# Sparse attention and graph convolution on one core: hub lookups, table scatters, tile clearing and short row blocks placed elsewhere in the order of work

## The chip, the core and the metric

The kernel runs on one core of a Trainium2 chip. Times are microseconds (us) of device time for one whole execution. The engines of the core are called PE (TensorE, matmul), DVE (VectorE), ACT (ScalarE), POOL (GpSimd) and SP (SyncE, which only issues transfers here). A time is the median of several executions; a profile is of one execution, whose own time is given beside its span.

## The reference, cut to what matters

There are 2708 rows of 1024 numbers, and a 0/1 matrix adj of 2708 x 2708 whose density falls with row and column, so that a few rows and columns at the front have many ones and some rows have none. All values are float32.

```
def layer0(x, adj):                       # attention over the ones of adj
    q, k, v = x @ W_q.T + b_q, x @ W_k.T + b_k, x @ W_v.T + b_v
    z = (q @ k.T) / sqrt(1024) * adj
    z = where(z == 0, -10000, z)
    return relu(softmax(z, axis=1) @ v)
def layer1(x, adj):
    return adj @ (x @ weight) + bias
x   = layernorm(x + layer0(x, adj))
out = layernorm(x + layer1(x, adj))
```

A row without ones gets the softmax of equal scores, which is the mean of all rows of v.

## The kernel before

**Numbers rather than masks.** The kernel never forms the full matrix of scores. With M the product of Wq and Wk, the score of row i and column j is a dot product of y_i = x_i M with x_j, so only the columns in a row's list are needed. The kernel builds those lists, sorts the rows by their number of columns into 22 blocks (NB) of up to 128 rows (the last block has 20), and for each block gathers column after column: one gather brings, for each of the 128 rows, the row of x which is its next column. Row blocks with long lists come first; the longest lists (the "hub") are cut into shares, which are worked on as a block of their own and joined later. Families: blocks 0 to 7 are the first family (FAMILY = 8) and 8 to 21 the second; each has its own table of lists in memory. The table of a family is written by scatters, one for each block of records (`records_out`, L650), and loaded back into the tile `tabs` (L660); `records_back` (L677) then makes the masks from it.

**The hub's lists.** `deal_hub` (L455 to L582) is a generator that is advanced a step at a time (`next(deal)`, L754 to L755) among the first y blocks. One of its steps looks up the hub's columns: 11 small gathers write the tile `found` (L566 to L568). The next one makes `valid_h`, `tab_h` and `less_h` from it (L570 to L574), and two permutation tiles `to_0` and `far_0` which don't depend on it (L576 to L581). Small tiles such as `found` and `at_i` come from the pool `lists`, which is given back before the tiles of the attention are laid out; pools that are laid out over it have to wait for the last use of what was there.

**Stages.** (1) Until about 150 us: M, and the lists of columns from adj. (2) The y blocks: `y_block` (L367) multiplies one block of 128 rows with M, in 16 matmuls of 128x512 (two halves of 8), and DVE adds a row `y_bc` while it empties each PSUM bank into `yo` (L320, called from L377). There are four such banks. SP stores `yo` to memory as `y_d` (L365). Blocks 0 to 7 stand in a first loop (L749), with lists and hub work between them; blocks 8 to 21 are the first steps of the list `steps` (L1129). The last block has its own form, `y_last` (L398). (3) Pairs: `steps` goes on with ten pairs of row blocks, whose weighted sums of x rows are turned (transposed on PE, L823) and multiplied with Wv by a seven-product scheme (`pair_products`, products at L306). (4) Layer 1 from about 764 us: sums of gathered rows of the new x (`sum_rows`, L1280), turned and multiplied with the layer's weights in ten `units`, with a normalisation and a scatter of the result (L810) one unit later.

**Attention jobs.** They are worked on beside the y blocks and pairs. A job (`attend` L918; `attend_one` L983; for the hub and block 0 `attend_shares` L1011) gathers the rows of y that belong to its block (`yg`, L428), which for the first family needs all of blocks 0 to 7 stored, then gathers x rows into a ring of nine tiles `g` (L434), makes one score per gathered tile on DVE (L904), a softmax, and the weighted sum `r` of the same tiles (first term on ACT at L959 or L1043, others on DVE at L961 or L1045). A tile of `g` is free again when its term of the sum is done. Because a gather leaves a lane alone where a row's list is shorter, the nine tiles are cleared once (L793 to L794) before their first use.

**What sets the order.** Each engine works its queue strictly in the order in which the program was laid out; there is one queue for POOL's gathers, scatters and loads. The order is set by a loop over `steps` (L1173) that keeps a credit of estimated time (`COST`, L1131) and advances jobs while there is credit. Parts under `tc.high_priority` are put ahead of ordinary ones by the scheduler. `follow(later, earlier)` (L421) makes one instruction wait for another; `products` holds the last matmul of every y block in the order of issue, so that `products[-2]` is the end of the block before the one issued last. `join` (L1152) advances hub and block 0 to their last steps, PE work at L1053 and L1063, a given number of steps after their sums are issued.

**The mean of x.** Rows without columns need the mean of all rows of x. `column_sums` (L415) makes it from the transposed x tiles on ACT, eight sums for each block, each behind one of that block's matmuls; `y_last` adds them up (`xbT`, L404 and L405), and `bcast_rows` (L1215) spreads the result over the partitions with transposes at L187.

**Rows without columns in layer 1.** The blocks named `last` (20 and 21) consist of such rows. In layer 1 they need only their own row of x1 plus the bias (`gather_x1`, L1301), a normalisation and a scatter (`finish1`, L1308); both are appended at i == 2 (L1365) and finished at the next unit, in the loop over units (L1352). The sum of the hub takes 11 gathers at i == 4 (L1363), behind those of the unit three further on.

## Time and profile before

| | |
|---|---|
| median of three runs | 1101.32 us (1097.92 to 1105.58) |
| profiled execution, own time | 1093.68 us |
| its span | 1092.0 us |
| PE busy | 983.0 us (90%) |
| DVE busy | 824.4 us (75%) |
| POOL busy | 484.5 us (44%) |
| ACT busy | 426.0 us (39%) |
| y matmuls (L374), busy | 300.8 us |
| scores (L904), 108 of them | 131.7 us, 1.219 us each |
| gathers of g in the attention (L434), 84 of them | 112.3 us, 1.337 us each |

A busy PE is not a PE at its peak, and the shares are averages over stages with different limits. In the lists of waits below, an engine and its line come first, then what ended the wait, then the sum of the waits in us, their number and the longest one. In timelines, each line is a start, a duration, the engine, the line of the kernel, the operation and its tiles; the bracket at the end gives the idle time just before it and what ended it. "issue" there means that the engine waited for nothing that the profile shows. The table by stretch gives the length of the stretch, then for each of PE, weight load, DVE, ACT and POOL the busy time and the number of instructions, then the granted clock, the share of the transfer engines and GB/s.

### The profile page before, as it was taken

To read this page: it belongs to the slowest core of one execution; us is meant where nothing else is said; L and a number is where in the kernel's file an instruction comes from. 1 tells how busy PE (TensorE), PEld (TensorE's weight loads), DVE (VectorE), ACT (ScalarE), POOL (GpSimd) and SP (SyncE) were. 2 spreads that over 40 slices of the span, in tenths; PEclk is the share of its full clock that TensorE was granted. 3 is DMA by queue.
4 is the path that set the end of the run, shared out by engine and by line. 5 is a ranking of instruction groups with operands and counts; after the bars stand their busy time and mean duration, and the time that the engine had idled before them with its cause. 6 is when DMAs were issued, how large, how long until landed. Compare 5 with 4: busy or idle time off the path is not lost.

```text
span 1092.0 us, 10690 instructions
## 1 busy us (share of the span) xinstructions
PE 983.0 (90%) x2761; PEld 463.0 (42%) x2761; DVE 824.4 (75%) x2038; ACT 426.0 (39%) x893; POOL 484.5 (44%) x530
## 2 busy tenths in 40 slices
PE   7999989999997999659999999999499885999993
PEld 6444444444333434225554444444244332445441
DVE  8999799953387998995799999645478865696532
ACT  4599994222032322222623444322322334333421
POOL 0000500057554555442465765110678776787400
PEclk9999989999999999889999999999799996999997
DMA  9688849956576867453447777225597697879711
GB/s 347 191 286 250 251 143 326 314 175 209 176 256 207 271 201 226 137 165 119 131 131 232 259 233 269 78 77 206 170 314 225 183 302 243 259 225 312 192 50 42
DMA packets 105781, 228.79 MB, mean 210 GB/s; under 512 B 22500, under 2 KB 49900, under 8 KB 105710
## 3 DMA queue, kind: packets, MB, share of 16 engines
q0 software_dynamic: 48192, 147.52, 42.5%
q1 hardware_dynamic: 57518, 80.50, 22.7%
q8 instruction: 23, 0.38, 0.1%
q14 instruction: 48, 0.39, 0.1%
HBM read 217.60 MB, written 33.68 MB: 230 GB/s over the span
## 4 chain that ended last, share of the span: by engine, by line
PE 28%; issue 19%; DVE 17%; POOL 12%; DMA 9%; ACT 1%; POOLq 0%; DVEq 0%; SPq 0%
PE po L306 23%; POOL g L434 6%; DVE junkv L904 2%; DMA g<-in_x_dram,tabs 2%; PE po L374 2%; DVE r L961 2%; POOL xr L428 1%; PE tr L823 1%; DMA g<-x_d,tabs 1%; POOL yg L428 1%; POOL tab_d L652 1%; DMA out_dram<-t,tabs 1%; DVE junkc L738 1%; DMA yg<-y_d,tabs 1%; DVE at_a L235 1%
## 5 line engine op out<-in xcount | busy, mean ns | idle before, releaser
L374 PE MATMUL po<-m,xt 128*128 128x512 f32 x672 | 300.8, 607 | 17.2 <-DVE yo L320 14.9
L374 PEld LDWEIGHTS po<-m,xt 128*128 128x128 f32 x672 | 128.7, 194 | 184.2 <-issue 153.9
L904 DVE SCALAR_TENSOR_TENSOR junkv<-yg,g 128x1024 uint8<-128x1024 f32 x108 | 131.7, 1219 | 44.8 <-DMA yg<-y_d,tabs 25.9
L306 PE MATMUL po<-t,s_all 128*128 128x512 f32 x320 | 148.2, 607 | 10.1 <-DVE xr L320 8.8
L434 POOL DMA_INDIRECT g<-in_x_dram,tabs x84 | 112.3, 1337 | 76.6 <-DVE r L961 19.0
L1295 DVE SCALAR_TENSOR_TENSOR r<-g,valid,r 128x1024 f32<-128x1024 f32 x77 | 98.0, 1280 | 29.2 <-DMA g<-x_d,tabs 26.7
L700 PE MATMUL po<-wk_o,wq_o 128*128 128x512 f32 x256 | 110.5, 592 | 0.0
L306 PEld LDWEIGHTS po<-t,s_all 128*128 128x128 f32 x320 | 61.2, 193 | 91.7 <-issue 72.8
L434 POOL DMA_INDIRECT g<-x_d,tabs x66 | 79.1, 1199 | 22.5 <-issue 16.8
L306 PE MATMUL po<-w,rT 128*128 128x512 f32 x160 | 74.2, 605 | 14.3 <-DVE t L1332 14.3
L417 ACT ACTIVATE junka<-xt 128x128 f32<-128x128 f32 x176 | 54.2, 308 | 82.2 <-PE po L374 61.5
L235 DVE FIND_INDEX8 at_a<-ones,a 128x8 uint16<-128x83 f32 (+3 forms) x132 | 82.6, 630 | 0.3 <-issue 0.3
L866 ACT ACTIVATE junks<-t,lnm 128x1024 uint8<-128x1024 f32 (+1 forms) x40 | 45.9, 1147 | 94.3 <-DVE lnm L864 93.1
L961 DVE SCALAR_TENSOR_TENSOR r<-g,pr,r 128x1024 f32<-128x1024 f32 x64 | 81.5, 1279 | 1.4 <-ACT r L959 1.2
L824 ACT COPY rT<-tr 128x512 f32<-128x512 f32 x76 | 41.2, 588 | 98.4 <-PE tr L823 97.7
L700 PEld LDWEIGHTS po<-wk_o,wq_o 128*128 128x128 f32 x256 | 48.3, 190 | 59.3 <-issue 58.6
L306 PE MATMUL po<-t,rT 128*128 128x512 f32 x160 | 73.0, 598 | 0.3 <-DVE t L320 0.3
L306 PE MATMUL po<-w,s_all 128*128 128x512 f32 x160 | 72.1, 592 | 0.0
L306 PE MATMUL po<-wv,s_all 128*128 128x512 f32 x160 | 71.9, 592 | 0.0
L306 PE MATMUL po<-wv,rT 128*128 128x512 f32 x160 | 70.7, 594 | 0.0
L879 ACT ACTIVATE t<-t,nmr,rstd 128x1024 f32<-128x1024 f32 (+1 forms) x40 | 49.0, 1238 | 49.5 <-DVE nmr L878 48.4
L810 POOL DMA_INDIRECT x_d<-t,tabs x22 | 25.9, 1175 | 75.0 <-ACT t L879 62.8
(352 smaller groups left out, 1425.8 us busy)
## 6 DMA issues: line engine op xcount, KB each, us to landing
xt<-in_xT_dram SPq DMA_DIRECT2D x21, 512.0 KB
y_d<-yo SPq DMA_DIRECT2D x21, 512.0 KB
a<-in_x_dram SPq DMA_DIRECT2D x21, 512.0 KB
a<-in_adj_dram SPq DMA_DIRECT2D x21, 413.5 KB
a<-in_adj_dram SPq DMA_DIRECT2D x21, 338.5 KB
a<-in_adj_dram SPq DMA_DIRECT2D x21, 263.5 KB
wq_i<-in_wqT_dram SPq DMA_DIRECT2D x8, 512.0 KB
wk_i<-in_wkT_dram SPq DMA_DIRECT2D x8, 512.0 KB
```

What stands on the lines that cost most here:

```text
L235: nc.vector.max_index(at[:n, i], ones[:n, :8], a[:n, cuts[i] + 8 * i:cuts[i + 1] + 8 * i + 8])
L306: put = nc.tensor.matmul(acc, a[:, k], w[:, k], start=start and k == 0, stop=stop and k == DC // 2 - 1, skip_group_check=True)
L374: put = nc.tensor.matmul(po, xts[b][:, c, :], m_q[c // 4][h][:, c % 4], start=(c == 0), stop=(c == DC - 1))
L417: put = nc.scalar.activation(junka, xts[b][:, c, :], AF.Copy, accum_out=xs[:, c, b:b + 1])
L434: nc.gpsimd.indirect_dma_start(out=dst[:n], out_offset=None, in_=src, in_offset=bass.IndirectOffsetOnAxis(ap=at, axis=0), bounds_check=N - ...
L700: nc.tensor.matmul(po, wq_o[i // 2][:, o, i % 2 * P:(i % 2 + 1) * P], wk_o[:, o, hs], start=(o == 0), stop=(o == DC - 1))
L824: nc.scalar.copy(rT[:, g * 4:g * 4 + 4, :], tr)
L866: nc.scalar.activation(junks[:n], t[:n], AF.Square, bias=nm[:n], accum_out=vs[:n])
L879: applied.append(nc.scalar.activation(t[:n], t[:n], AF.Identity, bias=nmr[:n], scale=rstd[:n]))
L904: nc.vector.scalar_tensor_tensor(junkv[:n], yg[:n, :D], scale, xg[:n], op0=ALU.mult, op1=ALU.mult, accum_out=s)
L961: nc.vector.scalar_tensor_tensor(r[:n], xg[j][:n], pr[:n, j:j + 1], r[:n], op0=ALU.mult, op1=ALU.add)
L1295: put = nc.vector.scalar_tensor_tensor(r[:n], xg[:n], ok[:n, j:j + 1], r[:n], op0=ALU.mult, op1=ALU.add)
```

## The change

Six edits:

- The 20-row block is multiplied before block 20 rather than after it, and the column sums of blocks 20 and 21 are both made inside `y_last`, behind the products of the block before. `xbT` is then made there.
- The 11 lookups of `found` are advanced from y block 5 to the step of y block 10, and each follows the end of block 8; what is made of `found` goes from block 7 to the step of block 13. `to_0` and `far_0` are made where the lookups had been. `found` and `at_i` are in the pool `const` instead of `lists`.
- The 14 scatters of the second family's table go from the steps of blocks 8 to 14 (two each) to those of blocks 11 to 17, and each pair follows the end of the block two steps back; `records_back(1)` goes from block 16 to block 19.
- The nine tiles of `g` are cleared by ACT (a copy scaled with 0) instead of by POOL, the first tile last.
- While y blocks are left, `join` waits two steps instead of one.
- In layer 1 one of the two blocks of `last` is appended at i == 4 and the other at i == 6.

```diff
@@ -376,7 +376,8 @@
                         firsts.append(put)
                 add(to[h], po, base[h])
             products.append(put)
-            column_sums(b, firsts)
+            if b != NB - 2:
+                column_sums(b, firsts)
             load_x()
             y_store(b, yo)
 
@@ -399,7 +400,8 @@
             n = rows[b]
             assert n <= HUB
             xt, yo = xts[b], yos[b % 3]
-            column_sums(b)
+            for c in (b, b - 1):
+                column_sums(c, [products[-1]] * (DC // 2))
 
             nc.vector.tensor_reduce(xbT, xs, AX.X, ALU.add)
             nc.vector.tensor_scalar_mul(xbT, xbT, 1.0 / N)
@@ -424,10 +426,10 @@
             tc.add_manual_dep(later.ins, earlier.ins.name, mybir.DependencyInfo(kind, mybir.DependencyReason.DATA),
                               reason="an engine's queue shall not stand still for a transfer")
 
-        def gather_at(src, at, n, dst, op=ALU.bypass):
-            nc.gpsimd.indirect_dma_start(out=dst[:n], out_offset=None, in_=src,
-                                         in_offset=bass.IndirectOffsetOnAxis(ap=at, axis=0), compute_op=op)
-            return dst
+        def gather_at(src, at, n, dst, op=ALU.bypass, put=False):
+            issued = nc.gpsimd.indirect_dma_start(out=dst[:n], out_offset=None, in_=src,
+                                                  in_offset=bass.IndirectOffsetOnAxis(ap=at, axis=0), compute_op=op)
+            return issued if put else dst
 
         def gather_slot(src, at, n, dst):
 
@@ -547,7 +549,7 @@
                                                accum_out=at[:, j:j + 1])
             nc.vector.tensor_add(at, at, q)
             nc.vector.tensor_scalar_min(at, at, float(P * KW - 1))
-            at_i = small("at_i", HUB_SLOTS, I32)
+            at_i = const.tile([P, HUB_SLOTS], I32, name="at_i")
             nc.vector.tensor_copy(at_i, at)
 
             row = small("row")
@@ -563,22 +565,22 @@
             nc.tensor.transpose(tr[:, 0, :], row.to_broadcast([P, P]), ident)
             nc.vector.tensor_scalar(alike, tr[:, 0, :], row, None, op0=ALU.is_equal)
             far_from(alike, far_h)
-            found = small("found", HUB_SLOTS)
+            nc.vector.tensor_copy(to_0, ident[:, HUB:])
+            nc.vector.tensor_add(to_0[:, :HUB], to_0[:, :HUB], ident[:, :HUB])
+            nc.vector.tensor_copy(far_0, ident)
+            nc.vector.tensor_add(far_0[:, :HUB], far_0[:, :HUB], ident[:, HUB:2 * HUB])
+            nc.vector.tensor_add(far_0[:, HUB:2 * HUB], far_0[:, HUB:2 * HUB], ident[:, :HUB])
+            far_from(far_0, far_0)
+            yield
+            found = const.tile([P, HUB_SLOTS], F32, name="found")
             for j in range(HUB_SLOTS):
-                gather_at(keys_d[:, :], at_i[:, j:j + 1], P, found[:, j:j + 1])
+                follow(gather_at(keys_d[:, :], at_i[:, j:j + 1], P, found[:, j:j + 1], put=True), products[-2])
             yield
-            nc.vector.tensor_scalar(valid_h, found, 0.0, None, op0=ALU.is_gt)
+            follow(nc.vector.tensor_scalar(valid_h, found, 0.0, None, op0=ALU.is_gt), products[-2])
             nc.vector.scalar_tensor_tensor(found, valid_h, -float(N + 1), found, op0=ALU.mult, op1=ALU.add)
             nc.vector.tensor_scalar_add(tab_h, found, float(N))
             far_from(valid_h, less_h)
             nc.vector.tensor_scalar_mul(less_h, less_h, -1.0)
-
-            nc.vector.tensor_copy(to_0, ident[:, HUB:])
-            nc.vector.tensor_add(to_0[:, :HUB], to_0[:, :HUB], ident[:, :HUB])
-            nc.vector.tensor_copy(alike, ident)
-            nc.vector.tensor_add(alike[:, :HUB], alike[:, :HUB], ident[:, HUB:2 * HUB])
-            nc.vector.tensor_add(alike[:, HUB:2 * HUB], alike[:, HUB:2 * HUB], ident[:, :HUB])
-            far_from(alike, far_0)
             yield
 
 
@@ -647,11 +649,13 @@
             nc.vector.tensor_scalar_add(rec[:, :, OFF], own[:, bs], float(-b0 * P))
             return f, nb, rec, pos_i
 
-        def records_out(f, nb, rec, pos_i, k0, k1):
+        def records_out(f, nb, rec, pos_i, k0, k1, behind=None):
             for b in range(k0, k1):
                 put = nc.gpsimd.indirect_dma_start(
                     out=tab_ds[f][:, :], out_offset=bass.IndirectOffsetOnAxis(ap=pos_i[:, b:b + 1], axis=0),
                     in_=rec[:, b, :], in_offset=None)
+                if behind is not None:
+                    follow(put, behind)
                 tc.declare_no_dep(put.ins, group=f"tab{f}", reason="disjoint rows: positions are unique")
                 tc.add_to_no_dep_group(f"tab{f}", put.ins)
             if k1 < nb:
@@ -751,7 +755,7 @@
                 list_columns()
                 done += 1
             y_block(b)
-            if b in (0, 1, 3, 4, 5, 7):
+            if b in (0, 1, 3, 4, 5):
                 next(deal)
             row_constants(len(c_ready))
             for _ in range({3: 3, 4: 3, 5: 2, 6: 3}.get(b, 0)):
@@ -788,10 +792,11 @@
 
             return gp.tile([P, D], F32, name="g", tag="g")
 
+        gs = [g_tile() for _ in range(G1)]
         with tc.high_priority(URGENT):
 
-            for _ in range(G1):
-                nc.gpsimd.memset(g_tile(), 0.0)
+            for g in gs[1:] + gs[:1]:
+                nc.scalar.activation(g, ones[:, :1].to_broadcast([P, D]), AF.Copy, scale=0.0)
 
 
         def gather(src, b, word, n):
@@ -1126,7 +1131,7 @@
         late_jobs = [7, 19, 18, 8, 8, 17, 8, 16, 11, 15, 10, 9, 14, 19, 13, 12, 18]
         late = set(late_jobs)
         jobs, late_jobs = jobs + late_jobs, len(late_jobs)
-        steps = [("y", b) for b in range(FAMILY, NB)]
+        steps = [("y", b) for b in list(range(FAMILY, NB - 2)) + [NB - 1, NB - 2]]
         steps += [("p", pairs[0]), ("mean", tuple(last))] + [("p", pair) for pair in pairs[1:]]
         COST = {"p": PAIR - EVICT + FLIP, "mean": 5.6, NB - 1: 2.0}
 
@@ -1177,7 +1182,7 @@
             pending = []
             credit += COST.get(kind, COST.get(b, STEP - Y_END))
             step[0] = i
-            join(i, 1)
+            join(i, 2 if left_y else 1)
             if kind == "y" and b == NB - 3:
                 (q11, q12), (q21, q22) = wv_q
                 follow(nc.vector.tensor_sub(q12, q12, q11), products[-2])
@@ -1201,9 +1206,11 @@
             if not left_y:
                 turn(i)
             if kind == "y":
-                if b < FAMILY + 7:
-                    records_out(*later_records, 2 * (b - FAMILY), 2 * (b - FAMILY) + 2)
-                if b == FAMILY + 8:
+                if b in (FAMILY + 2, FAMILY + 5):
+                    next(deal)
+                if 3 <= b - FAMILY < 10:
+                    records_out(*later_records, 2 * (b - FAMILY - 3), 2 * (b - FAMILY - 3) + 2, products[-2])
+                if b == FAMILY + 11:
                     records_back(1)
                 (y_last if b == NB - 1 else y_block)(b)
                 left_y -= 1
@@ -1362,9 +1369,9 @@
             if i == 4:
                 sum_rows("hub")
             pending = list(zip(unit, *work1(unit, *turned1.pop(i), xrs.pop(i))))
-            if i == 2:
-                for b in last:
-                    pending.append((b, gather_x1(b), None))
+            if i in (4, 6):
+                b = last[i // 2 - 2]
+                pending.append((b, gather_x1(b), None))
         for p in pending:
             finish1(*p)
         for pool in (cp, wv_pool, wm_pool):
```

## The prediction

> **What bounds the kernel now.** I read the page's slices first, then the waits of TensorE (PE), the stretch table, and the timelines where a wait ends. The profiled execution took 1093.68 us, its span 1092.0, so 1.7 us lie outside; the median of the three runs, 1101.32, is 7.6 us above it.
>
> ```profile
> PE   7999989999997999659999999999499885999993
> DVE  8999799953387998995799999645478865696532
> POOL 0000500057554555442465765110678776787400
> ```
>
> Each digit is 27.3 us. PE is nearly full, but not in slices 17 to 19 (about 464 to 519 us, between the y blocks and the pairs), nor in slices 29 and 32 to 34 of layer 1. Slices 8 to 10 show a VectorE (DVE) with little to do (3, 3, 8), just ahead of a stretch where it is full. What PE waited for:
>
> ```profile
> PE po L374 <- DVE yo L320: 14.9, 9, 3.1
> PE po L306 <- DVE t L1332: 14.3, 1, 14.3
> PE tr L823 <- DVE r L1292: 13.8, 1, 13.8
> PE tr L187 <- DVE nms L952: 12.6, 1, 12.6
> PE mm L1063 <- DVE den L1059: 7.7, 1, 7.7
> ```
>
> The columns are us in total, times, longest. Four of these lines (first, second, fourth, fifth) are open to this change. Per stretch (PE, PEld, DVE, ACT, POOL busy):
>
> ```profile
> 225.00:290.40 65.40, 65.05 (x155) 29.06 (x154) 18.78 (x39) 11.27 (x56) 48.84 (x49) 1.00 0.55 175
> 290.40:487.50 197.10, 161.37 (x412) 68.36 (x411) 178.32 (x288) 55.60 (x250) 97.39 (x69) 0.95 0.66 209
> ```
>
> From 290.4 to 487.5 DVE is busy 178.3 of 197.1 us: it bounds the y blocks, since its attention work (L904, L961, L1045) stands in one queue with the additions that empty PE's banks. In the 65 us before, it works 18.8. So what matters is when its first score can start:
>
> ```profile
> 242.77 8.11 POOL L794 MEMSET g<- 128x1024 f32 x9
> ...
> 283.18 0.98 POOL L428 DMA_INDIRECT xr<-in_x_dram,tabs  x1 [0.30 <-issue]
> 284.34 1.17 POOL L660 DMA_DIRECT2D tabs<-tab_d  x1 [0.18 <-issue]
> 285.81 1.00 POOL L428 DMA_INDIRECT yg<-y_d,tabs  x1 [0.30 <-issue]
> ...
> 290.44 1.23 DVE L904 SCALAR_TENSOR_TENSOR junkv<-yg,g 128x1024 uint8<-128x1024 f32 x1 [23.27 <-DMA yg<-y_d,tabs]
> ```
>
> The trace puts the 23.27 us down to the transfer of yg, but that took 4.6 us from its issue. GpSimd (POOL) issued it late: ahead of it stand 11 found gathers (226.4 to 242.8), the clearing of nine g tiles, and 14 scatters, nearly all 0.30 us after one another. The data was there sooner: block 7's y was sent at 260.33, and such a 512 KB transfer takes 4.2 us (231.17 in the chain), so it lay whole at 264.5.
>
> The end of the y blocks, and the stall of layer 1:
>
> ```profile
> 486.61 0.69 DVE L320 TENSOR_TENSOR yo<-po,y_bc 128x512 f32<-128x512 f32 x1
> ...
> 488.65 0.16 DVE L405 TENSOR_SCALAR xbT<-xbT 128x8 f32<-128x8 f32 x1
> ...
> 488.87 1.97 PE L187 MATMUL tr<-ident,xbT 128*128 128x128 f32 x8 [12.59 <-DVE nms L952]
> ```
> ```profile
> 901.11 1.02 POOL L810 DMA_INDIRECT out_dram<-xr,tabs  x1 [3.66 <-ACT xr L879]
> ...
> 906.60 1.41 POOL L428 DMA_INDIRECT xr<-x_d,tabs  x1 [1.86 <-ACT xr L1305]
> ```
> ```profile
> 910.96 2.08 PE L306 MATMUL po<-w,rT 128*128 128x512 f32 x2 [14.35 <-DVE t L1332]
> ```
>
> PE had finished the y matmuls at 476.28 and waited 12.59 us for xbT (L405 ended at 488.8; the named nms is its neighbour). In layer 1 POOL waits 3.66 us at the output scatter of a block of `last`, with the gathers of the next sums behind it; DVE then waits 4.49 and 2.33 us for those (at 904.05 and 907.67), and PE 14.35.
>
> **What the Trainium skill says.** "PSUM — Partial Sum Buffer", section Engine vs sequencer instructions: the queues of ScalarE, VectorE and GpSimd are strict FIFOs. The trace agrees: yg at 285.81 went behind scatters that it doesn't need, 21 us after its data. "DMA: Bandwidth & Descriptors", section Issuing engine by pattern: indirect transfers are GpSimd's; here all of L428, L434, L652 and L810 are. So what the change moves stays in that queue, only later. "SBUF — State Buffer", section Who interferes with whom: DVE and GpSimd share a port pair that one holds for a whole instruction. The trace agrees: during the memsets two small DVE operations (L570, L578) took 6.54 and 6.52 us.
>
> **The change, part by part.**
>
> *Clearing on ScalarE.* Nine copies of 128x1024; the same shape takes 1.147 us (L959), so 10.4 us against 8.11. They stand behind column sums of block 6 (about 233), and the tiles' space comes free when the list work ends, about 236 to 237: done by about 247. ScalarE was busy 11.3 of 65.4 us there, so this is hidden; only the column sums behind come later. The nine gathers of g follow at about 238 to 250 and are whole 6 us later, before 264.5.
>
> *Found gathers and scatters later.* With 11 found, nine memsets and 14 scatters gone from its front, POOL reaches yg before the data does. First score: 264.5 + 4.6 = 269.1, against 290.44: 21.3 us sooner.
>
> *Their price.* 25 issues of 0.96 + 0.30 = 1.26 us, 31.6 us, now lie among the g gathers that feed DVE through nine tiles. The order of instructions shows eight found directly behind the third yg, then three in twos and ones, then seven pairs of scatters. Before, the first refill of g was issued 9.8 us after the first score (300.28); now yg (about 273), then eight found (10 us): about 16.3 us after it, 6.5 more. A pair delays what is behind it by 2.5 us; POOL was busy 97.4 of 197 us, so half of that should find slack, and the waits for a block's end, two steps back, are over by then. Before, DVE waited 16.3 us for g in this stretch. I take e = 12 us more; bounds 5 (the first burst alone) and 31.6 (all of it lost).
>
> *DVE's queue.* In the new order, ahead of the last addition yo, there are 3 L904 (1.31 with the read of its sum) and 5 L1045 (1.28) fewer, one L1040/L1041 (0.9), L1065 to L1068 and three small ones fewer, five small ones of valid_h (0.8) more: 3.9 + 6.4 + 0.9 + about 1.1 - 0.8 = 11.5 us less. That work falls into 489 to 524, where DVE idled 17.8 us in gaps (3.98, 0.16, 0.84, 1.92, 2.57, 1.87, 6.50); so pairs hardly see it, but it takes up that slack.
>
> *y_last before block 20, mean sooner, L1063 later.* L405 stands ahead of the last addition, so the 12.59 and the 7.7 us of PE go. What is late next is pair 0: s_all and the additions of t stand behind left-over scores and sums, about 6.5 us of PE. End of the y blocks: 269.1 + (486.6 - 290.4) - 11.5 + e = 453.8 + e. PE's own floor is below: block 8 starts near 259.5, 13 blocks of 13.74 and the small one give 442. Flips of pair 0 began 4.0 us after the last addition (490.63); now they can begin at once but cost those 6.5. Gain at the pairs: 490.6 - (453.8 + e + 6.5 - 3.6) = 33.9 - e = 22 us. The pairs (PE waits 1.4 us in 490 to 764) move as a whole.
>
> *Layer 1.* After the 13.83 at its start, PE idles 27 us until 1075, of which the stall is 14.35, and the matmuls after stalls run slow (5.40 us for eight instead of 3.60). The two rows' scatters and gathers, 4 issues (5 us) and their 11 us of waits on POOL (3.66, 1.86, 2.30, 1.98, 1.04), leave the place before the hub's gathers (L1363). Behind them, a wait of up to 7 us can come back before the next units' gathers, for xr has two buffers. I take 12 us of gain; bounds 20 (stall, 3.40 and slow matmuls gone) and -4.
>
> *Sum.* 22 + 12 = 34: 1093.7 - 34 = 1059.7 in the profiled execution, and 7.6 more for the median: 1067.
>
> **Rivals.**
> 1. *Only the y stretch gains.* The stall of layer 1 returns at the new place of the rows (unit 8 and 9 feed just in time). For it: POOL is 7 to 8 tenths full there. Against it: after the hub's sum PE ran from 983 to 1075 without a wait. Time 1101.3 - 22 = 1079.
> 2. *The queue gives the head start back.* e = 31.6, nothing hidden: the pairs begin 2 us sooner and layer 1 gains 8 to 12. Time 1101.3 - 2 - 9 = 1090.
> 3. *GpSimd becomes the bound, slower.* Found and scatters not only take 31.6 us: each of seven pairs and the found burst also stands waiting for its block's end with the g gathers behind it. Price 31.6 + 8 x 3.0 (about the longest such wait on g now, 3.3) = 55.6; 33.9 - 55.6 = -22, and layer 1 unchanged: 1123. It decides from e = 34, or 46 if layer 1 gains its 12. For it: DVE already waits on g there. Against it: the blocks waited for ended a step earlier.
> A change that does nothing (block 7's y, not the queue, held yg) is excluded by the 21 us between the two.
>
> **How the numbers follow.** Forecast 0.55, with its own range 1054 to 1081 (e from 5 to 20, layer 1 from 4 to 20); rival 1 0.2, rival 2 0.13, rival 3 0.12. All of the forecast and of rival 1, and a third of rival 2, are faster by over 1% (below 1090.3): 0.79; the rest of rival 2 is within 1%: 0.09; rival 3: 0.12. One per cent is about what a measurement of this kernel can tell from no change. Range 1050 to 1091.
>
> **What will show it.** First L904 near 269; no 12.6 wait at L187 and none of 7.7 at L1063; DVE's waits on g in the y blocks up from 16 to about 28; flips of pair 0 near 466 to 470; no wait of 14 us on L1332, PE idle in layer 1 down from 27 to about 12. Wrong if the first score comes after 280, if DVE's waits on g pass 50, or if a stall over 10 us comes back behind the rows of `last`.

## The result and the profile after

The changed kernel took 1087.51 us in the median of four runs (1084.31 to 1089.95), the kernel before 1101.6 beside it (the three runs given above and a fourth): 14.1 us less, ratio 0.987 with an interval of 0.9826 to 0.9913. In a second series (r1 below) the ratio was 0.9912 (0.9884 to 0.994), 10.8 us less, and in a third (r13) 0.9922 (0.9892 to 0.9953), 7.6 us less. So the direction was right and the size was not: 34 us were forecast, 8 to 14 came.

The profiled execution of the changed kernel took 1088.43 us, its span 1086.7. The slices of its page, PE, DVE and POOL, show the repair and its limits:

```profile
PE   7999979999999998498999999999599899669993
DVE  8989699961688888796999999545568876966332
POOL 0000500031666645243565755111678676767300
```

Counted from 1, DVE's digits 10 to 12 are now 1, 6, 8 where they were 3, 3, 8: its dense stretch starts earlier. POOL does little in digits 9 (3) and 10 (1), ahead of yg. But PE has a 4 in slice 17 and two 6s in slices 35 and 36. The waits of PE name them:

```profile
PE tr L841 <- DVE part L1302: 16.1, 1, 16.1
PE po L395 <- DMA xt<-in_xT_dram: 15.9, 1, 15.9
PE tr L828 <- DVE r L1299: 14.2, 1, 14.2
PE po L374 <- DVE yo L320: 7.2, 4, 3.5
PE po L306 <- DVE t L320: 7.1, 5, 4.9
```

The 12.6 (mean's turning), the 7.7 (hub's joining) and the 14.3 of layer 1 are gone, as the edits intended; the waits for the additions of the y blocks fell from 14.9 to 7.2. In their place stand two waits of 16 us that were not there before: at L395, the matmuls of the 20-row block, and at L841, the turning of the hub's rows in layer 1. (L841, L828, L1302 and L909 are L836, L823, L1295 and L904 of the kernel before; other lines are shifted in the same way, by up to seven, and by one or two more in runs that add a tile.) Per stretch:

```profile
225.00:290.40 65.40, 65.40 (x157) 29.34 (x156) 29.68 (x74) 25.49 (x88) 24.00 (x22) 1.00 0.66 204
290.40:487.50 197.10, 173.06 (x463) 76.76 (x462) 163.72 (x265) 52.91 (x237) 110.77 (x88) 0.94 0.64 201
```

In the first stretch DVE does 29.7 us instead of 18.8; ScalarE does 25.5 instead of 11.3 with the clearing. The start of the attention, on POOL and DVE:

```profile
247.66 0.99 POOL L436 DMA_INDIRECT g<-in_x_dram,tabs  x1 [0.30 <-ACT junka L419]
268.96 0.95 POOL L430 DMA_INDIRECT yg<-y_d,tabs  x1 [20.32 <-issue]
270.22 0.95 POOL L430 DMA_INDIRECT yg<-y_d,tabs  x1 [0.30 <-PE po L374]
277.69 1.68 POOL L430 DMA_INDIRECT yg<-y_d,tabs  x1 [6.53 <-DVE scores L916]
279.67 0.97 POOL L430 DMA_INDIRECT found<-keys_d,at_i  x1 [0.30 <-issue]
```
```profile
273.39 1.23 DVE L909 SCALAR_TENSOR_TENSOR junkv<-yg,g 128x1024 uint8<-128x1024 f32 x1 [3.61 <-DMA yg<-y_d,tabs]
...
296.88 1.23 DVE L909 SCALAR_TENSOR_TENSOR junkv<-yg,g 128x1024 uint8<-128x1024 f32 x1 [8.16 <-DMA g<-in_x_dram,tabs]
```

POOL now stands idle for 20.32 us. SP sends block 7's y at 262.94, and yg follows 6.0 us later: that it waits for this store is inferred from the order, for the trace names no releaser here (in r6, below, it puts the same wait down to `y_d<-yo`). Behind the third yg come eight lookups, and the first refill of g reaches DVE late: 8.16 us.

**One scale for all kernels.** The first stage, which the change does not touch, ended 144 to 151 us after the start, with a wait of PE for y_bc of 3.8 to 9.7 us. So places are given from S, the last turning before the y blocks (of u_col, L187): 144.64 before, 147.33 after. The trace of before was also a quick execution, 7.9 us under the median of its four runs, and that of the changed kernel 0.9 us over its own, which is why the spans differ by 5.3 us and the medians by 14.1. Such spread goes in part with the granted clock: of 29 runs of the kernel before beside r9 to r12, the six with the lowest clock (0.952 to 0.954) took 1097.9 to 1105.6 us, the five with the highest (0.961 to 0.963) 1092.7 to 1097.2; the trace of before had 0.962, that of the changed kernel 0.958. From S, in us:

| kernel | first score | last yo addition | first turning of pair 0 | first turning of layer 1 | layer 1 to the end | median of runs |
|---|---|---|---|---|---|---|
| before | 145.8 | 342.0 | 346.0 | 633.2 | 314.1 | 1101.6, then 1096.3 to 1097.9 |
| changed | 126.1 | 328.7 | 328.4 | 625.6 | 313.8 | 1087.51 |
| r1, changed again | 125.6 | 330.1 | 329.9 | 624.6 | 315.2 | 1087.08 |
| r2, own tile | 125.0 | 321.2 | 319.7 | 610.8 | 313.1 | 1077.12 |
| r3, hub later | 125.6 | 329.4 | 329.2 | 626.0 | 303.4 | 1081.58 |
| r4, lookups early | 132.4 | 329.6 | 329.4 | 623.4 | 310.9 | 1081.84 |
| r5, r2 and r3 | 125.2 | 323.2 | 320.9 | 613.4 | 307.5 | 1069.09 |
| r6, r5 and lookups early | 129.2 | 317.7 | 316.0 | 606.6 | 307.7 | 1064.5 |
| r7, rows at i == 2 | 126.5 | 332.6 | 332.4 | 627.1 | 315.6 | 1092.79 |
| r8, short block last | 127.6 | 327.8 | 330.8 | 618.3 | 312.2 | 1080.79 |
| r9, scatters early | 139.0 | 338.0 | 337.8 | 632.2 | 313.0 | 1094.7 |
| r10, clearing on POOL | 128.1 | 332.5 | 332.3 | 626.6 | 313.6 | 1087.26 |
| r11, head start alone | 125.1 | 333.2 | 337.2 | 624.1 | 317.0 | 1092.37 |
| r12, r6 and scatters early | 149.9 | 331.5 | 327.1 | 620.9 | 302.0 | 1078.77 |
| r13, changed again | 125.1 | 330.7 | 330.5 | 625.2 | 315.0 | 1088.71 |
| r14, r7 again | 126.0 | 331.4 | 331.2 | 627.8 | 317.2 | 1091.37 |
| r15, r6 with rows at i == 2 | 129.0 | 317.8 | 316.4 | 606.6 | 319.5 | 1077.03 |

The medians of r1 to r15 come from series with their own runs of the kernel before (medians 1096.34 to 1097.88), and are compared below with r1's 1087.08, so that a difference of 1 or 2 us between series says nothing; r13 and r14 ran on one chip and are compared with each other.

S itself is not the same in all: it comes at 147.7 to 150.6 in the five kernels with an own tile (r2, r5, r6, r12, r15) and at 144.0 to 147.3 in the others. On average that is 4 us later, which the places from S leave out and the medians contain. No run shows why.

### The profile page after: what moved, and what is told of

The parts are those of the page before. It is cut to its first block, busy times and chain, and to the rows that moved or that the text cites. A ratio compares the mean times of both kernels' runs of the same rounds, so it can differ in the third digit from the quotient of the medians.

```text
span 1086.7 us, 10683 instructions
## 1 busy us (share of the span) xinstructions
PE 983.2 (90%) x2761; PEld 463.9 (43%) x2761; DVE 820.4 (75%) x2038; ACT 432.3 (40%) x902; POOL 469.7 (43%) x521
## 4 chain that ended last, share of the span: by engine, by line
PE 26%; issue 20%; DVE 15%; DMA 12%; POOL 11%; ACT 1%; SPq 0%; POOLq 0%; DVEq 0%
PE po L306 18%; POOL g L436 6%; PE po L374 5%; DVE junkv L909 4%; DMA g<-x_d,tabs 3%; DVE r L966 3%; DMA g<-in_x_dram,tabs 2%; PE tr L828 1%; POOL xr L430 1%; DVE t L320 1%; PE po L395 1%; DVE yo L320 1%; DMA yg<-y_d,tabs 1%; DVE junkc L742 1%; DMA a<-in_adj_dram 1%
## 5 line engine op out<-in xcount | busy, mean ns | idle before, releaser
L374 PE MATMUL po<-m,xt 128*128 128x512 f32 x672 | 297.6, 604 | 7.2 <-DVE yo L320 7.2
L909 DVE SCALAR_TENSOR_TENSOR junkv<-yg,g 128x1024 uint8<-128x1024 f32 x108 | 131.8, 1220 | 37.6 <-DMA g<-in_x_dram,tabs 21.8
L306 PE MATMUL po<-t,s_all 128*128 128x512 f32 x320 | 147.4, 604 | 8.9 <-DVE r L1302 4.4
L436 POOL DMA_INDIRECT g<-in_x_dram,tabs x84 | 105.2, 1252 | 57.0 <-issue 16.2
L1302 DVE SCALAR_TENSOR_TENSOR r<-g,valid,r 128x1024 f32<-128x1024 f32 x77 | 98.2, 1281 | 24.0 <-DMA g<-x_d,tabs 16.4
L306 PEld LDWEIGHTS po<-t,s_all 128*128 128x128 f32 x320 | 61.2, 193 | 90.1 <-issue 72.1
L436 POOL DMA_INDIRECT g<-x_d,tabs x66 | 76.5, 1158 | 22.5 <-issue 18.3
L306 PE MATMUL po<-wv,s_all 128*128 128x512 f32 x160 | 75.3, 615 | 5.9 <-DVE t L320 4.9
L306 PE MATMUL po<-t,rT 128*128 128x512 f32 x160 | 74.5, 609 | 1.5 <-DVE t L1339 0.9
L306 PE MATMUL po<-w,rT 128*128 128x512 f32 x160 | 72.5, 599 | 0.0
L306 PE MATMUL po<-w,s_all 128*128 128x512 f32 x160 | 72.0, 593 | 0.0
L306 PE MATMUL po<-wv,rT 128*128 128x512 f32 x160 | 70.5, 592 | 0.0
L231 ACT ACTIVATE junk<-a 128x2756 uint8<-128x2756 f32 (+1 forms) x22 | 55.0, 2502 | 8.8 <-DMA a<-in_adj_dram 2.4
```

The source lines that it names most:

```text
L231: nc.scalar.activation(junk[:n], a[:n], AF.Sign, accum_out=cnt[:n, b:b + 1])
L306: put = nc.tensor.matmul(acc, a[:, k], w[:, k], start=start and k == 0, stop=stop and k == DC // 2 - 1, skip_group_check=True)
L374: put = nc.tensor.matmul(po, xts[b][:, c, :], m_q[c // 4][h][:, c % 4], start=(c == 0), stop=(c == DC - 1))
L436: nc.gpsimd.indirect_dma_start(out=dst[:n], out_offset=None, in_=src, in_offset=bass.IndirectOffsetOnAxis(ap=at, axis=0), bounds_check=N - ...
L909: nc.vector.scalar_tensor_tensor(junkv[:n], yg[:n, :D], scale, xg[:n], op0=ALU.mult, op1=ALU.mult, accum_out=s)
L1302: put = nc.vector.scalar_tensor_tensor(r[:n], xg[:n], ok[:n, j:j + 1], r[:n], op0=ALU.mult, op1=ALU.add)
```

## The two new waits, read from the traces

The stall at L395, on PE, SP and POOL of the changed kernel:

```profile
449.81 5.05 PE L395 MATMUL po<-m,xt 128*32 128x256 f32 x64 [15.90 <-DMA xt<-in_xT_dram]
```
```profile
432.70 0.33 SPq L365 DMA_DIRECT2D y_d<-yo  x1
447.00 0.38 SPq L297 DMA_DIRECT2D xt<-in_xT_dram  x1
```
```profile
438.24 1.29 POOL L436 DMA_INDIRECT g<-in_x_dram,tab  x1 [4.91 <-ACT r L1048]
...
441.94 1.73 POOL L436 DMA_INDIRECT g<-in_x_dram,tab  x1 [0.81 <-DVE r L1050]
444.28 1.73 POOL L436 DMA_INDIRECT g<-in_x_dram,tab  x1 [0.61 <-DVE r L1050]
446.01 0.96 POOL L296 MEMSET xt<- 128x1024 f32 x1
```

The load of the 20-row block's transposed x was issued at 447.00, straight behind a clearing of its tile, which is a GpSimd memset in `load_x` (L296), written for short blocks. That memset stands in POOL's queue behind gathers of g, and each of those waits for DVE or ACT to free a tile; the memset itself follows the last of them without a pause. In the kernel before the same memset came at 452.00 and nobody noticed, because the 20-row block was multiplied last. One block sooner, PE stands at it.

Layer 1, on PE of the changed kernel:

```profile
939.84 1.04 PE L828 MATMUL tr<-ident,r 128*128 128x128 f32 x8
940.71 3.60 PE L306 MATMUL po<-w,rT 128*128 128x512 f32 x8
960.37 0.60 PE L841 MATMUL tr<-to_h,part 128*128 128x32 f32 x2 [16.06 <-DVE part L1302]
```

The hub's sum was ready sooner than before: its turning came 187.5 us after layer 1's first turning, against 205.1. But PE was at the place 16 us earlier still. The stretch table, for the products of L306 alone, from the first turning to the hub's and from there on (length, busy, number), first the kernel before, then the changed one:

```profile
777.80:982.90 205.10, 165.17 (x362) 0.94 0.80 245
982.90:1092.00 109.10, 85.66 (x198) 0.94 0.49 149
```
```profile
772.90:960.30 187.40, 151.22 (x336) 0.94 0.83 259
960.30:1086.70 126.40, 99.22 (x224) 0.92 0.49 142
```

14 us of products (26 records; the trace has two for each matmul of the program) now stand behind the hub's turning instead of ahead of it, and the 14.35 us stall ahead of it is gone. PE therefore arrives too early, waits, and does those products later.

The two causes have different weight. Without its wait, PE would have been at the hub's turning 203.4 us after the first turning before, and 171.4 in the changed kernel: 32.0 us sooner. Its idle time ahead of that place fell by 18.0 us (25.4 to 7.4), and 14.0 us of products changed sides. The sum, ready 17.6 us sooner, makes up for the first and not for the second. That order comes with the edit: in r7 and r14 below, where both rows stand at i == 2 again, 362 records are ahead once more, and PE waits 0.9 and 1.7 us.

```profile
771.90:977.40 205.50, 164.83 (x362) 0.94 0.81 247
```

This line is r7's, from the first turning to the hub's.

## The experiments

**r1: the changed kernel again.** No edit.

> The changed kernel once more, for its spread and for a second profile of it. Theory A (the traces as they stand): the end of the y blocks near 475 and layer 1 as long as before the change, about 314 us; time 1084 to 1090. Rival (the one profile of before was a lucky one and layer 1 did get shorter): layer 1 of this second profile is shorter than 308 us.

Median 1087.08, layer 1 315.2 us, the same two waits (16.0 and 16.7 us). Theory A holds: layer 1 did not get shorter.

**r2: own tile for the 20-row block.** `load_x` also ends one block sooner, and `y_last` and its column sums read the new tile.

```diff
-            if n < P:
-                nc.gpsimd.memset(xt, 0.0)
...
+        xt_last = xa.tile([P, DC, HUB], F32, name="xt_last", bufs=1)
+        nc.gpsimd.memset(xt_last, 0.0)
+        nc.sync.dma_start(out=xt_last[:, :, :rows[-1]], in_=xT[:, (NB - 1) * P:].rearrange("(c p) n -> p c n", p=P))
```

> Gives the 20-row block its own small tile of transposed x, cleared and loaded at the start, so that the clearing no longer stands in GpSimd's queue behind gathers. Theory A (the move of the 20-row block ahead of block 20 turned that clearing into a stall of TensorE of 15.9 us that delays the end of the y blocks): the stall is gone, the last addition of the y blocks comes 5 to 12 us sooner, time 7 us below the changed kernel, 1078 to 1083. Rival (VectorE is the bound there and the stall is hidden): the stall goes, the waits on the additions of VectorE grow by as much, the time moves by less than 2 us.

1077.12, 10.0 below r1, a little more than theory A had. PE's waits:

```profile
PE tr L843 <- DVE part L1304: 16.1, 1, 16.1
PE tr L830 <- DVE r L1301: 13.7, 1, 13.7
PE tr L187 <- ACT y_bc L188: 9.6, 1, 9.6
...
PE po L396 <- DVE yo L321: 6.8, 1, 6.8
```

The matmuls of the short block wait 6.8 us for a bank now, not 15.9 for data. The last addition comes 7.5 us sooner than in the changed kernel, layer 1 starts 14.8 us sooner. The rest of the y edits is all there: from S, layer 1 begins 22.4 us sooner than before. Not all of the 14.8 need be the wait. The mean granted clock from S to pair 0 was 0.98 here, and 0.96 and 0.95 in the two traces of the changed kernel; PE's busy time in that stretch was 302.1, 303.7 and 305.7 us, so the clock can account for 2 to 4 us.

**r3: the hub's unit one place later.**

```diff
-(4, 10), (6, 0), (5, 11), (12, 13)]
+(4, 10), (5, 11), (6, 0), (12, 13)]
...
-            if i == 4:
+            if i == 5:
                 sum_rows("hub")
```

> Layer 1 takes the unit with the hub's rows (6, 0) one place later, behind (5, 11), and the hub's sum one unit later. Theory A (the stall of layer 1 did not go, it moved from the output scatter to the hub's sum, whose 29 gathers are too many for one unit of matmuls): the 16 us wait at the hub's turning falls under 4 us and the time by 8 to 15 us, to 1073 to 1080. Rival (GpSimd's queue bounds all of layer 1): the wait shows at another turning, the time moves by less than 3 us.

1081.58, 5.5 below r1, less than the 8 to 15 expected, though layer 1 itself is 10.4 to 11.8 us shorter (303.4). PE's wait at the hub:

```profile
988.48 0.38 PE L841 MATMUL tr<-to_h,part 128*128 128x32 f32 x2 [1.43 <-DVE nmr L883]
```

16 us became 1.4, and apart from the 13.8 at layer 1's first turning, which all traces have, no wait at another turning is longer than 2.9. The rival falls: GpSimd doesn't bound all of layer 1; PE had too little other work between (424 records stand ahead of the hub's turning now, against 336). The trace is of a quick execution, 4.7 us under the median of its runs.

**r4: lookups early.**

```diff
-            if b in (0, 1, 3, 4, 5):
+            if b in (0, 1, 3, 4, 5, 7):
...
-                if b in (FAMILY + 2, FAMILY + 5):
+                if b == FAMILY + 5:
```

> The eleven lookups of found are advanced at y block 7 instead of block 10, so that they lie in GpSimd's idle 20 us ahead of the first yg; all else is as in the changed kernel. Theory A (eight lookups behind the third yg cost VectorE the 8.2 us wait for g that follows its first scores): that wait falls under 2 us, waits of VectorE for g in the y blocks from 27 to about 19 us, time 3 to 8 us lower, 1080 to 1085. Rival (TensorE's 15.9 us wait for the 20-row block sets the end of the y blocks, so that a faster VectorE buys nothing): VectorE waits for TensorE instead, time within 2 us of the changed kernel.

1081.84, 5.2 below r1. The 8.2 us wait is gone (the longest of that kind is 2.3), and DVE's waits for g fell from 27.1 to 20.5 us. But yg was issued later, so the first score came 6.3 us later, and the last addition at the same place; PE still waited 16.1 us for the short block. Layer 1 begins 1 to 2 us sooner, and is 3 to 4 us shorter, which the edit doesn't explain. So the time fits theory A and the trace only half of it; r6 asks again without the short block's wait.

**r5: r2 and r3 together.** Edits as above.

> Both repairs on the changed kernel: the 20-row block in its own tile, loaded at the start, and the unit with the hub's rows one place later. Theory A (the predicted 22 us of the y stretch and 12 us of layer 1 are there, and two new waits of 16 us took most of them): the two gains add, 10 and 8 to 12 us below the changed kernel, 1065 to 1071, which is where the prediction stood. Rival (the two waits cover each other, since layer 1 waits on a queue that starts sooner): less than 13 us below the changed kernel, over 1074.

1069.09, 18.0 below r1: ratio 0.9736 (0.9693 to 0.978). Theory A holds: the gains of 10.0 and 5.5 (8.0 beside r2) add. This is 32.5 us below the 1101.6 that stood beside the changed kernel's first series, 27.6 below its own series.

**r6: r5 with the lookups at y block 6.**

```diff
-            if b in (0, 1, 3, 4, 5):
+            if b in (0, 1, 3, 4, 5, 6):
...
-                if b in (FAMILY + 2, FAMILY + 5):
+                if b == FAMILY + 5:
```

> As the run before, and the eleven lookups of found advanced at y block 6, ahead of the first gathers of g, with nothing of them behind the third yg. Theory A (the burst of lookups costs VectorE some 8 us of wait for g, and with the 20-row block's wait gone VectorE bounds the y stretch): no wait of 8 us for g after the first scores, time 4 to 8 us below the run before. Rival (TensorE's floor bounds the y stretch by now): VectorE waits for TensorE in its place, time within 2 us of the run before.

1064.5, 4.6 below r5 and 22.6 below r1; ratio to before 0.9701 (0.9656 to 0.9747), the fastest of all. DVE's waits in the y stretch:

```profile
DVE yo L321 <- PE po L375: 18.1, 2, 14.2
DVE junkv L911 <- DMA g<-in_x_dram,tabs: 8.8, 7, 3.0
DVE junkv L911 <- DMA yg<-y_d,tabs: 7.9, 1, 7.9
DVE junkv L911 <- DMA g<-in_x_dram,tab_h: 7.2, 4, 4.6
DVE junkv L911 <- DMA g<-in_x_dram,tab: 2.9, 3, 1.4
```

18.9 us for g, against 27.1 in the changed kernel; the first score 4.0 us later than in r5 and the last addition 5.5 sooner. Theory A holds. The wait of 14.2 lies before the first score, and is put down to PE, which had however filled that bank (the first half of block 7) at 255.4, 8.6 us before the addition began at 263.9. In the changed kernel the same addition follows at once (255.3 and 255.4). So block 7's y goes out late here, and POOL stands 12.59 us ahead of yg, for `y_d<-yo`: that is the later first score. r9 comes back to it.

**r7: both rows of `last` at i == 2 again.**

```diff
-            if i in (4, 6):
-                b = last[i // 2 - 2]
-                pending.append((b, gather_x1(b), None))
+            if i == 2:
+                for b in last:
+                    pending.append((b, gather_x1(b), None))
```

> The changed kernel with its layer 1 edit undone: both blocks of rows without columns appended at i == 2. Theory A (that edit only moved the stall): the 14 us wait on L1332's additions is back, the hub's wait is under 4 us, layer 1 lasts 312 to 317 us, time within 3 us of the changed kernel. Rival (the prediction's step, 12 us of gain): layer 1 10 us longer, 1095 to 1099.

The waits of PE in layer 1:

```profile
PE po L306 <- DVE t L1339: 14.0, 1, 14.0
PE tr L828 <- DVE r L1299: 13.7, 1, 13.7
```

The stall is back in its old place and the hub's turning waits 0.9 us. Layer 1 lasts 315.6 us, against 313.8 and 315.2: the edit moved the stall, as theory A has it. The median, 1092.79 over sixteen runs from 1084.56 to 1100.62, is however 5.7 above r1, more than theory A allows and less than the rival's 8 to 12. r13 to r15 take this up.

**r8: the 20-row block last again.**

```diff
-        steps = [("y", b) for b in list(range(FAMILY, NB - 2)) + [NB - 1, NB - 2]]
+        steps = [("y", b) for b in range(FAMILY, NB)]
...
-            for c in (b, b - 1):
-                column_sums(c, [products[-1]] * (DC // 2))
+            column_sums(b)
```

> The changed kernel with its first edit undone: the 20-row block after block 20, its column sums and the mean at the end. Theory A (the edit's new wait for the transposed x costs more than the wait for the mean that it removes, once VectorE is ahead): no wait of 16 us for the transposed x, a wait of 2 to 8 us at the mean's turning, pairs 3 to 8 us sooner, time 1079 to 1085. Rival (the prediction's step: the waits of 12.6 and 7.7 us come back): pairs begin 6 to 12 us later, 1092 to 1100.

1080.79, 6.3 below r1. The mean's turning waits 7.9 us and the short block 4.9 for a bank:

```profile
PE po L374 <- DVE yo L320: 9.1, 7, 5.0
PE tr L187 <- DVE turn L1069: 7.9, 1, 7.9
PE po L394 <- DVE yo L320: 4.9, 1, 4.9
```

Pair 0's first turning is 2.4 us later than in the changed kernel, but the pairs take 287.5 us instead of 297.2, and layer 1 starts 7.3 us sooner. So the first edit, as it stands, costs 6 us. With its tile cared for (r2) the median is 4 us lower than with the edit left out, but the intervals of r2 and r8 (0.9782 to 0.9877, 0.9804 to 0.99) overlap.

**r9: the scatters at blocks 8 to 14 again.**

```diff
-                if 3 <= b - FAMILY < 10:
-                    records_out(*later_records, 2 * (b - FAMILY - 3), 2 * (b - FAMILY - 3) + 2, products[-2])
-                if b == FAMILY + 11:
+                if b < FAMILY + 7:
+                    records_out(*later_records, 2 * (b - FAMILY), 2 * (b - FAMILY) + 2)
+                if b == FAMILY + 8:
```

> The changed kernel with its scatter edit alone undone: the second family's 14 scatters in the steps of blocks 8 to 14, without a wait, so that they stand around the first gathers of g, ahead of yg, where GpSimd idled 20 us; the lookups stay behind the third yg. Theory A (the scatters cost VectorE some waits among the gathers, and little in the idle time): first score 2 to 6 us later against the start of the y blocks, waits of VectorE for g 27 down to 18 to 22 us; the time within 3 us of the changed kernel. Rival (e was mostly scatters): waits for g under 14 us, time 6 us or more below it.

1094.7, 7.6 above r1: neither theory. DVE's waits for g fell only from 27.1 to 21.5, as theory A said, but the first score came 13 us later:

```profile
264.95 0.69 DVE L320 TENSOR_TENSOR yo<-po,y_bc 128x512 f32<-128x512 f32 x1 [16.69 <-remote]
272.12 1.29 DVE L320 TENSOR_TENSOR yo<-po,y_bc 128x512 f32<-128x512 f32 x2 [6.48 <-remote]
285.83 1.23 DVE L909 SCALAR_TENSOR_TENSOR junkv<-yg,g 128x1024 uint8<-128x1024 f32 x1 [12.42 <-DMA yg<-y_d,tabs]
```

An addition of block 7 stood for 16.69 us until something that the trace calls remote and doesn't name; block 7's y was stored at 273.44 instead of 262.94, and yg had to wait for it. The scatters had all been issued by 267.5. What held the addition is open. It was not the bank, which was full at 254.4, 10.6 us before. The same addition stood 8.6 us in r6 and 8.3 in r15, after eleven lookups in a row, 22.3 in r12, and not at all in the changed kernel, in r4, r5, r10 and r11. PE too paused in r9 and r12 for nothing that the profile shows (2.8 and 10.7 us). What the four late ones share, and the others lack, is such a row of ten or more directly ahead of the nine gathers of g (in r4 the lookups stand behind these gathers); no run tests whether that is the cause.

**r10: clearing on GpSimd again.**

```diff
-            for g in gs[1:] + gs[:1]:
-                nc.scalar.activation(g, ones[:, :1].to_broadcast([P, D]), AF.Copy, scale=0.0)
+            for g in gs:
+                nc.gpsimd.memset(g, 0.0)
```

> The changed kernel with the nine tiles cleared by GpSimd again. Theory A (GpSimd has 20 us idle ahead of yg, so the clearing costs nothing on either engine): first score, end of the y blocks and time the same within 2 us. Rival (the clearing is part of the head start): first score 6 to 8 us later, time 4 to 8 us higher.

1087.26, r1 within 0.2 us; first score 2.0 to 2.5 us later from S, last addition 2.4 to 3.8, layer 1 at 626.6 against 624.6 to 625.6. Theory A holds for the time, and is 1 or 2 us off in the places: with the lookups and scatters gone, POOL has the time, and ScalarE's part of the change is worth nothing.

**r11: the head start alone** (lookups, scatters and clearing changed; edits of r7 and r8, and `join(i, 1)`).

> The kernel before with only the edits of lookups, scatters and clearing: the 20-row block last, one step for the hub's joining, both rows at i == 2. Theory A (the head start is real, and is what the whole change brings): first score 19 to 21 us sooner than before, the waits at the mean's turning and the hub's joining still there, layer 1 starts 10 to 16 us sooner, time 10 to 16 us below the kernel before, as low as the changed kernel or lower. Rival (the queue gives it back): less than 4 us below the kernel before.

1092.37, 5.3 below its series' kernel before; ratio 0.9942 (0.9908 to 0.9976), between the theories. The first score is 20.7 us sooner than before, the last addition 8.8: DVE's waits for g rose to 29.0, and the rest is lost there. The waits at the mean (11.8) and the hub's joining (8.5) are still there, layer 1 begins 9.1 us sooner. r8, which adds the later joining and the layer 1 edit, begins layer 1 another 5.8 us sooner; the later joining was not run alone.

**r12: r6 with the scatters early.** Edit of r9 on r6.

> The fastest so far (own tile, hub later, lookups early) with the scatters early as well: nothing but gathers left among the first scores. Theory A (idle time of GpSimd is filled, but yg then comes some 5 us late): first score 4 to 7 us later than there, waits for g under 12 us, time within 3 us of it, 1061 to 1067. Rival (each issue taken out of the loop counts in full, 17.6 us): 8 us or more below it.

1078.77, 14.3 above r6: both theories miss. The same unnamed wait as in r9, 28.5 us long here, and the first score at 149.9. It says that the scatters cost time there, and no more.

**r13, r14: the changed kernel, and r7, once more on one chip.** No edit, and the edit of r7.

> The changed kernel once more, beside the next two on one chip. 1084 to 1090.

> The changed kernel with both rows without columns at i == 2, once more. Theory A (the edit only moves a stall from the additions to the hub's turning): within 3 us of r13. Rival (it is worth a few us even so): 4 to 7 us above r13.

1088.71 (1086.91 to 1089.5) and 1091.37 (1085.09 to 1097.86): 2.7 us apart, ratios to before 0.9922 (0.9892 to 0.9953) and 0.9947 (0.9927 to 0.9967), whose intervals overlap. Layer 1 lasts 315.0 and 317.2 us. Theory A holds: in the changed kernel the edit is worth 2.7 us in this pair and 5.7 in r7 against r1, neither clear of the spread.

**r15: r6 with both rows at i == 2.** The edit of r7 on r6.

> The fastest kernel (own tile, hub's unit later, lookups early) with both rows at i == 2. Theory A (the edit's 12 us are real where the hub's turning doesn't take them back): a stall of about 14 us on L1339's kind of addition comes back in layer 1, which lasts 8 to 13 us longer than the 307.7 there, time 8 to 13 us above the fastest kernel, 1072 to 1078. Rival (layer 1 is bound by GpSimd's queue, wherever the rows stand): within 3 us of it.

1077.03, 12.5 above r6. The y blocks and pairs are the same to 0.4 us, and layer 1 is 11.8 us longer (319.5 against 307.7). PE's waits in layer 1:

```profile
PE po L307 <- DVE t L1341: 14.4, 1, 14.4
PE tr L830 <- DVE r L1301: 13.8, 1, 13.8
```

The stall is back at its 14 us, and the hub's turning waits only 0.4. So the edit is worth its 12 us where the hub's unit stands later, and 3 to 6 at most where it doesn't. The later unit alone is worth nothing either: layer 1 with it and with the rows at i == 2 lasts longer (319.5) than in the kernel before (314.1).

## Why the prediction was wrong, step by step

**The head start: right.** First score 21.3 us sooner by the prediction, 19.7 and 20.2 from S by the two traces. POOL's queue and not the data held yg: POOL now stands idle 20.32 us ahead of it instead.

**Clearing on ScalarE at no cost: right.** 8.60 us for nine instead of 10.4, done at 244.6, and hidden. It was worth nothing either (r10): POOL had the time.

**The price e = 12 us in DVE's waits: right.** DVE waited 27.1 us for g where 28 was forecast, and in r11, which has the head start alone, 20.7 us at the first score became 8.8 at the last addition: 11.9 us. The eight lookups behind the third yg make the largest single part (8.2 us), and r6 gets that part back. The time of 25 issues, given as 31.6 us, is 25 x 1.26 = 31.5.

**DVE's queue 11.5 us shorter: nearly right.** From the first score to the last addition DVE was busy 177.4 us before and 167.4 in the changed kernel, 10.0 less; three scores and five terms of the sum moved behind it, as said. In r11, which lacks the other edits, it was 177.9.

**The end of the y blocks: right but for one step.** 486.6 - 453.8 - 12 = 20.8 us sooner was the sum for the last addition. r2 has 20.8 from S, and layer 1 begins 22.4 us sooner there, against the 22 predicted. The changed kernel itself has 13.3 and 7.6. What failed is the step "*y_last before block 20, mean sooner, L1063 later*", which counted only the waits that the move removes (12.59 and 7.7), and pair 0's stalls. It did not follow the moved block's own input back: its load waits for a memset in POOL's queue, and POOL's queue waits for DVE. The floor of 442 for PE was worked out as if that load were free. The move's own price was 15.9 us of PE wait, and taking it away is worth 10 us of the time (r2).

**Pair 0: right in kind.** 6.5 us were set aside; the pairs took 297.2 and 294.7 us instead of 287.3, 7 to 10 more, and 291.1 in r2. Without the first edit they took 287.5 (r8). That PE comes to the pairs further ahead of DVE fits this and its 7.1 us of waits for `t`, but was not tested.

**Layer 1: wrong.** The step took 12 us for the stall's going and allowed "a wait of up to 7 us" behind it. The stall went, as said, and the sums ended 17.6 us sooner from layer 1's start. But the step asked only when the sums are ready, not when PE gets to them: without the stall, and with 26 records of products moved behind the hub's turning, PE came 16 us too soon. Layer 1 lasted 313.8 and 315.2 us against 314.1. PE's idle time after the first turning, 27 us before and forecast at about 12, was 24.4 and 26.6. With one more unit of products ahead of that turning it falls to 14.8 to 18.2 (r3, r5, r6, r12), and r15 against r6 has the edit's 12 us by itself: 11.8. So the step could give about its size, under a condition that the prediction did not see. Against the kernel before, layer 1 is then 6.4 to 12.1 us shorter, 10.7 and 12.1 in r3 and r12, whose traces are quick executions, and 6.6 and 6.4 in r5 and r6. Rival 1 had named this outcome, a stall come back elsewhere, but put it behind the rows of `last` and not at the hub; so did the prediction's own sign of being wrong.

Put together: 22 + 12 were predicted, 7.6 to 8.6 and -1.1 to 0.3 came in the traces from S (r13: 8.0 and -0.9). With both waits repaired (r5) layer 1 starts 19.8 us sooner than before and is 6.6 shorter, and the median is 27.6 below its series' kernel before, within 7 us of the 34. Of the forecast and its rivals, the 1090 of rival 2 is nearest to what was measured, but by luck: in it the queue gives the head start back, with 31.6 us more of waits, and 10.8 came. Rival 3, which ended slower, has nothing for it: no pause of POOL ahead of one of the 14 scatters was longer than 0.31 us, so their waits for a block's end did not add to their issue times.

**Two readings of the slices.** The prediction puts PE's gap in slices 17 to 19, 464 to 519 us; the 6 and the 5 of its line stand in 17 and 18, 437 to 491 us. DVE's 3, 3, 8 are slices 10 to 12, not 8 to 10. The waits that it then took from the timelines are right, and no sum used the slices.

## What to carry to other kernels

When a step is moved earlier, follow each of its inputs back through every queue that it passes, down to the clearing of a tile: an instruction that was harmless because its user came last becomes the user's wait. When a stall is removed ahead of a meeting point of two engines, work out the arrival of both, from the order of the changed program and not of the old one: the engine that is freed arrives sooner too, work of its own may have changed sides, and the time is gained only if it has other work to do before the meeting. And read a lone profile against the spread of the timed runs: here the two traces differed by 5.3 us and the medians by 14.1.

## What was not expected of the hardware

Nine copies of one broadcast column into 128x1024 tiles took 8.60 us on ScalarE as a group; one took 1.038 us by itself, where a scaled copy of a full 128x1024 tile took 1.147 us (L959 before). GpSimd's memset of the same tile took 0.969 us, nine of them 8.11.

Two small operations of DVE stood 6.54 and 6.52 us during those nine memsets, until the last of them ended at 250.88: they were held for the rest of the row, not for one memset of 0.969 us. In r10, with the memsets on GpSimd at another time, three more stood 1.68 to 2.42 us, until that row ended at 236.8; one of them, at `far_h`, took 0.21 us in the changed kernel.

In r9 and r12, where GpSimd issued nine to ten scatters of small records in a row ahead of the gathers, an addition of DVE stood 16.69 and 28.45 us for a releaser that the trace calls remote. The kernel before issues ten such scatters in a row too, later on, and shows no such wait.
